# A cast of the last rows moved ahead of a slot's last exponentials, with other moves in the fill and the end, in a cross-attention kernel

## Chip, core and metric

The kernel runs on one core of one Trainium2 chip. The metric is the device time of one launch in microseconds (us). Engines are named as in the profile: PE (matmul) and PEld (its weight loads), DVE (vector), ACT (scalar), POOL (GpSimd) and SP, which here only issues DMAs.

## What is computed

For each of B = 32 pictures there are 512 query rows of 640 channels (x) and 77 context rows of 1024 channels. There are 20 heads of 32 channels, and the softmax runs over the 77 context rows (the reference has further branches for rows after the 77th; there are none here).

```python
q, k, v = heads(x @ wq), heads(ctx @ wk), heads(ctx @ wv)
p = softmax(q @ k.T / sqrt(32))
out = merge(p @ v) @ wo + bo + x
```

All is fp32. The kernel forms each product from pairs: a high part (a cast to the matmul's reduced fp32 type) and a low part (the value minus its high part), and adds three products, high x high, high x low and low x high.

## The kernel before

**Stages.** First all keys and values are computed from the context in five groups of columns (lines 294 to 383) and parked in DRAM (k_dram, v_dram). In the third of these groups the five blocks of the output weights wo are loaded, split into pairs and written to DRAM as pairs (split_wo, line 318); they are loaded again later (line 759). Then come N = 160 **slots** (slot, line 701): slot n = 5b + j treats four of picture b's heads (j = 0 to 4). Slots 1 to 7 are the **fill**, when no finished attention is there to be projected; from slot 8 on (has_out) every slot has the same load. Function end (line 845) drains the last pieces.

**One slot.** PE makes the scores of four row tiles (line 478; scores 0 to 3), the queries of the next slot (443), the attention product of slot n-4 (573: six passes, four ahead of scores 3 and two behind) and a piece of an earlier picture's output projection (622). DVE takes each score tile's negated maximum (486). ACT does 16 exponentials (496), four per score tile ("exps 0" to "exps 3"), each with its sum. Then:

- sums (506, DVE) takes the reciprocals; for j = 4, 0 and 1 it stands on DVE right behind exps 3, for j = 2 and 3 in the next slot. normalize (513, POOL) multiplies.
- transpose_p (520, DVE) transposes to z; four DMAs write z to pd in DRAM (527). load_p (536, 537) reads pd back, turned, as raw: one DMA of 512 KB for 256 of the 320 rows of probabilities, and one of 128 KB for the 64 **last rows**. load_p(n-3) is issued in slot n, and its raw is used in slot n+1.
- cast_p (544, 545, ACT) casts first the last rows, then the rest (128x1024; "the large cast") to the high parts pp; rest_p (551, DVE) and last_p (558, POOL) make the low parts. In the fill POOL does the large cast.
- copy_a (583, ACT) moves half of the attention product out of PSUM, add_a (588, DVE, two adds) sums it, high_a (599, ACT) and low_a (604, DVE) split the sum into the pair at, which the projection reads. copy_a and add_a of a product are in its own slot, around exps 3; high_a and low_a at the start of the next.
- split_q (454 ACT, 458 POOL, 460 DVE) splits the next slot's queries; split_x (263 ACT, 264 POOL) splits five blocks of the next picture's x in slots j = 2 and 3.
- finish (654, DVE) adds the projection to the residual xr, which frees one of two PSUM banks po, and sends full tiles to the output.

**What sets the order.** The order on each engine is the order of the calls in slot, written by hand (manual_schedule). Every engine, and SP's queue of DMA issues, works strictly in that order: an instruction that waits holds up all that stand behind it. Tiles with bufs=1 or 2 add waits for the last reader.

On ACT, a slot with j < 4 begins with last-rows cast, large cast, high_a, and ends with copy_a, exps 3. DVE ends it with sums, then add_a (where j = 4, 0 or 1). On SP, raw's two loads stand behind the four writes of pd and half of the loads of keys or values (refill).

Of the kernel before, what the change touches and what calls it, by code (L numbers as in the profile page):

```python
# [8 lines left out]
F32 = mybir.dt.float32  # L9
FPR = mybir.dt.float32r  # L10
# [41 lines left out]
def kernel(  # L52
# [46 lines left out]
    v_dram = dram.tile([NT + KPAD - NKEY, HPC, NC_, 3, HD], FPR, name="v_dram")  # L99
    wo_dram = dram.tile([P, NC_, 2, C], FPR, name="wo_dram")  # L100

# [3 lines left out]

    def load_weights(w, k0, kn, permuted=True, queues=(nc.sync,) * 4, tag="wraw"):


        raw = kvw.tile([P, 2, C], F32, tag=tag, name="wraw", bufs=3 if tag == "wraw" else 2)
        if permuted:  # L110
            rows = w.rearrange("(q c i) n -> q i c n", q=4, i=Q)
            for q, queue in enumerate(queues):
                queue.dma_start(raw[q * Q : (q + 1) * Q, :kn], rows[q, :, k0 : k0 + kn])
        else:
            rows = w.rearrange("(c p) n -> p c n", p=P)
            nc.sync.dma_start(raw[:, :kn], rows[:, k0 : k0 + kn])
        for k in range(kn):
            wraws[id(w), k0 + k] = raw[:, k]

    def split_weights(dst, w, k, scale=None):  # L120

        part = wraws.pop((id(w), k))
        if scale is not None:
            nc.scalar.mul(part, part, scale)
        split(dst[:, 0, :], dst[:, 1, :], part)
# [81 lines left out]
    def split_keys(g, j):  # L207
        g0, gn = GROUPS_KV[g]
        ks = kvt.tile([P, 2, G], FPR, tag="ks", name="ks")
        split(ks[:, 0, :gn], ks[:, 1, :gn], pks.pop(j)[:, :gn])  # L210
        engine = nc.gpsimd if g + 1 < len(GROUPS_KV) else nc.sync
        j0 = GROUPS[GROUP_OF[j]][0]
        engine.dma_start(
            k_dram[GROUP_OF[j]][:, :, j - j0, g0 : g0 + gn].bitcast(F32), ks[:, :, :gn].bitcast(F32)
        )
# [28 lines left out]

    def load_x(b, quarters=range(4), queue=nc.sync):

        if b not in xss:
            xss[b] = xpool[0].tile([P, S // Q, C // 4], F32, tag="xs", name="xs")
        xs = xss[b]
        src = x[b].rearrange("(a j) (q u) -> q j a u", j=Q, q=4)  # L250
        for q in quarters:
            queue.dma_start(xs[q * Q : (q + 1) * Q, :, :], src[q])

# [63 lines left out]

    def split_wo():
        k = len(split_ks) - NC_
        split_ks.append(k)  # L320
        ws = kvw.tile([P, 2, C], FPR, tag="ws", name="ws", bufs=2)
        split_weights(ws, wo, k)
        nc.sync.dma_start(wo_dram[:, k].bitcast(F32), ws.bitcast(F32))

    load_context(1, NK)
# [4 lines left out]
    for g in range(LAST):  # L330
        for j in range(NC_):
            if g or j > 2:
                values_of(g, j, psk)
            if not g and j < 3:
                split_keys(0, j)
            if not g and j == 2:
                continue
            if j == 1:
                context(g + 1, 0)
            if not g and j == 3:  # L340
                split_values(0, 2)
                split_keys(0, 3)
            if j == 3:
                continue
            if j == NC_ - 1:
                context(g + 1, 1, 2)
                if not g:
                    split_keys(0, 4)
                split_values(g, 3, (None, split_wq, split_wo, None)[g])
                context(g + 1, *range(3, NK))  # L350
                if g + 1 == LAST:
                    kvw.release()
                    kvc.release()
                    xpool.append(
                        ctx.enter_context(
                            tc.tile_pool(name="xpool", bufs=1, reuse_waits="tile")
                        )
                    )
                    load_x(0)
            split_values(g, j, (None, split_wq, split_wo, None)[g])  # L360
        if g + 1 < LAST:
            load_context(g + 2, NK)
            if g < 2:
                for k in range(0, NC_, 2):
                    load_weights((wq, wo)[g], k, min(2, NC_ - k), permuted=g == 0)
            for k in range(NK):
                for j in range(NC_):
                    keys(g + 1, j, k)
            for j in range(NC_):
                split_keys(g + 1, j)  # L370
# [3 lines left out]
    for c in range(NC_):  # L374
        split_x(0, c)
    load_x(1, queue=nc.gpsimd)

# [16 lines left out]

    bias = main.tile([P, C], F32, name="bias")
    kbs, vbs, pnb = [], [], []
# [8 lines left out]
    qts = [main.tile([P, 3, S], FPR, name=f"qt{n}") for n in range(2)]  # L405
    z = main.tile([P, NBLK, NQ, Q], F32, name="z")
    for g, (j0, nj) in enumerate(GROUPS):
        vb = main.tile([P, nj, 2, 2, P], FPR, name=f"vb{g}")
        vbs.append(vb)

# [10 lines left out]
    def copy_keys(g):  # L421
        kb = kbs[g]
        nc.gpsimd.tensor_copy(kb[:64, 0], kb[:64, 1].bitcast(F32))
        nc.gpsimd.tensor_copy(kb[64:, 3], kb[64:, 2].bitcast(F32))

    def load_values(b, g, segments=SEGMENTS):
# [90 lines left out]
    def transpose_p(n):  # L517

        pn = pnb[n % 2]
        nc.vector.transpose(  # L520
# [12 lines left out]
    def load_p(n):  # L533
# [4 lines left out]
        raws[n] = raw  # L538

    def cast_p(n, shared=False):  # L540

        raw = raws[n]
        pp = late[0].tile([P, 5, S], FPR, tag="pp", name="pp", bufs=1)
        nc.scalar.copy(pp[:64, 4, :], raw[:64, 2, :])  # L544
        (nc.gpsimd.tensor_copy if shared else nc.scalar.copy)(pp[:, 0:2, :], raw[:, 0:2, :])  # L545
        pps[n] = pp

# [66 lines left out]
    def add_bias(b, t):  # L614
        nc.gpsimd.tensor_tensor(xrs[b, t], xrs[b, t], bias, ALU.add)  # L615

# [59 lines left out]

    WO = {1: (0, 1, 2), 5: (3,), 6: (4,)}
    wos = []

    def take(m):  # L680
# [20 lines left out]
    def slot(n, beside=()):  # L701
# [9 lines left out]
        if not filling:  # L711
            refill(b, j, 0)
        copied = {1: 1, 4: 0 if more else None}.get(j)
        if copied == 0 and has_out:
            copy_keys(copied)
            copied = None
        if taken is not None and j != NC_ - 1:
            cast_p(taken, filling)
        if n - 1 in takes:
            high_a(takes[n - 1])  # L720
        if taken is not None and j == NC_ - 1:
            cast_p(taken, filling)
        bias_now = j in BIAS and b >= BIAS[j][0]
# [7 lines left out]
        if has_out and j in (1, 2):  # L731
            normalize(n - 1, rss.pop(n - 1))
        if taken is not None:
            last_p(taken)
        if copied is not None:
            copy_keys(copied)
# [11 lines left out]
        if j != NC_ - 1 and n - 1 in takes:  # L748
            low_a(takes[n - 1])
        if taken is not None:  # L750
            rest_p(taken)
        if n == LATE + 2:
            nc.sync.dma_start(bias, bo.unsqueeze(0).to_broadcast([P, C]))
        if n >= LATE:
            load_p(n - LAG + 1)
        if filling:
            refill(b, j, 0)
        for k in WO.get(n, ()):
            nc.sync.dma_start(wos[0][:, k].bitcast(F32), wo_dram[:, k].bitcast(F32))
        refill(b, j, 1)  # L760
# [3 lines left out]
        if j in RESIDUAL and b >= RESIDUAL[j][0]:  # L764
            load_residual(b - RESIDUAL[j][0], RESIDUAL[j][1])
        exps(n, 1, *s)
        for i in turns[0]:
            transpose_x(b + 1, i)
# [10 lines left out]
        if early:  # L779
            piece(bo_, first)  # L780
            if j == 4:
                values(taken, 0, 4)
                s3 = scores(n, 3)
                values(taken, 4, 6)
            finish()
        if not ahead:
            transpose_p(n - 1)
        if ahead:
            split_q(n + 1)
            if parted:  # L790
# [27 lines left out]
        else:  # L818
# [3 lines left out]
            if taken is not None:  # L822
                values(taken)
        if len(beside) > 0:
            context_values(LAST, beside[0], psv)
        finish()
        for i in turns[1]:
            transpose_x(b + 1, i)
        if taken is not None:
            copy_a(taken)  # L830
        for c in xsplits[1]:
            split_x(b + 1, c)
        exps(n, 3, *s)
        if has_out and j in (4, 0, 1):
            rss[n] = sums(n)
        if taken is not None:
            add_a(taken)
        if len(beside) > 1:
            context_values(LAST, beside[1], psv)
        if has_out:  # L840
# [4 lines left out]
    def end():  # L845
# [3 lines left out]
        load_p(N - 3)  # L849
        load_values(last, 1)  # L850
        load_residual(last - 1, 3)
        piece(last - 1, 4)
# [4 lines left out]
        last_p(N - 4)  # L857
        rest_p(N - 4)
        transpose_p(N - 1)
        add_bias(last - 1, 2)  # L860
        load_p(N - 2)
        piece(last - 1, 5)
# [73 lines left out]

    load_keys(0, 0)
    queries(0, 0, NC_)
    split_q(0)
    copy_keys(0)  # L940
    for vb in vbs:
        nc.gpsimd.memset(vb.bitcast(F32), 0.0)
    context_values(LAST, 0, psv)
# [56 lines left out]
```

## Time and profile before

| | us |
|---|---|
| median of 3 runs | 1950.41 |
| lowest, highest | 1945.75, 1954.95 |
| the profiled execution | 1956.04 |
| its span (first to last instruction) | 1954.3 |

The granted PE clock over the profiled span is 0.993 of full speed. In the profile's views a row of "waits" says which engine stood idle at which line, and what ended the idle time: total us, times, longest. A row of the timeline has start and length in us, engine, line and tiles; a bracket at its end is the idle time before it and what ended it. A row of the windows has the busy time of each engine, the granted PE clock and the share in which the DMA engines were busy.

### The profile page before, as it was taken

The page shows a single profiled execution, that of the slowest core. Times are in us where ns is not written, and L with a number is a line of the kernel's source. Part 1 is how long each engine was busy: PE and PEld are TensorE (multiplying, and loading weights), DVE is VectorE, ACT ScalarE, POOL GpSimd, SP SyncE. Part 2 cuts the span into 40 slices and gives each one's busy share as a digit, 9 for nine tenths or more (in the row PEclk, how much of TensorE's full clock was granted, in tenths as well). Part 3 has the DMA queues.
Part 4 walks back from the last instruction along what each step waited for, and adds up shares of the span by engine and source line. Part 5 has one row for each costly group of instructions (what it writes and reads, how often), then busy time and mean ns, then how long its engine had stood idle before and what let it go on. Part 6 is the DMA issues. An engine that isn't in the chain of part 4 may idle for free.

```text
span 1954.3 us, 37691 instructions
## 1 busy us (share of the span) xinstructions
PE 1902.4 (97%) x10332; PEld 1663.2 (85%) x10332; DVE 1638.7 (84%) x2494; ACT 1532.9 (78%) x6206; POOL 1376.5 (70%) x1264
## 2 busy tenths in 40 slices
PE   9999997999999999999999999999999999999998
PEld 7888886888888888888888888888888888888887
DVE  4444447899999989989999999999999999999995
ACT  3232247888899889888888888989988889889883
POOL 1000057888888888878888787888888888788874
PEclk9999998999999999999999999999999999999999
DMA  9878868898898988888888888988889898888875
GB/s 188 197 190 251 190 184 207 216 232 227 227 237 227 223 227 225 228 219 231 223 235 226 227 225 227 235 231 232 221 234 229 229 229 225 227 223 228 230 201 168
DMA packets 570657, 431.39 MB, mean 221 GB/s; under 512 B 199440, under 2 KB 479120, under 8 KB 570448
## 3 DMA queue, kind: packets, MB, share of 16 engines
q1 hardware_dynamic: 566832, 416.36, 84.6%
q0 software_dynamic: 3520, 12.45, 1.8%
q8 instruction: 86, 1.41, 0.3%
q14 instruction: 123, 1.01, 0.2%
q10 hardware_dynamic: 96, 0.16, 0.0%
HBM read 247.17 MB, written 181.64 MB: 219 GB/s over the span
## 4 chain that ended last, share of the span: by engine, by line
PE 43%; POOL 15%; DMA 13%; DVE 9%; ACT 7%; issue 7%; SPq 5%; POOLq 0%; DVEq 0%; ACTq 0%
PE po L622 11%; PE pq L443 11%; DMA raw<-pd 8%; PE pk L191 7%; PE pv L191 7%; POOL pn L513 5%; PE pa L573 4%; PE sc L478 4%; ACT pn L496 3%; POOL pp L558 3%; POOL qt L458 3%; POOL xt L264 2%; DMA xs<-in_x_dram 2%; DVE nm L486 2%; DVE pp L551 2%
## 5 line engine op out<-in xcount | busy, mean ns | idle before, releaser
L496 ACT ACTIVATE pn<-sc,nm 128x77 f32<-128x77 f32 x2560 | 794.3, 331 | 58.0 <-DVE nm L486 53.1
L622 PE MATMUL po<-wo_s,at 128*128 128x320 f32 x3840 | 629.1, 312 | 17.9 <-DVE xr L654 13.2
L443 PE MATMUL pq<-xt,wq_s 128*128 128x512 f32 x2400 | 631.5, 403 | 1.2
L622 PEld LDWEIGHTS po<-wo_s,at 128*128 128x128 f32 x3840 | 575.6, 188 | 47.8 <-DVE xr L654 26.5
L496 ACT ACTIVATION_READ_ACCUMULATOR pn<-sc,nm 128x1 f32 x2560 | 539.1, 211 | 0.0
L513 POOL TENSOR_TENSOR pn<-pn,rs 128x616 f32<-128x616 f32 x320 | 448.4, 1419 | 116.4 <-DVE rs L506 105.2
L443 PEld LDWEIGHTS pq<-xt,wq_s 128*128 128x128 f32 x2400 | 429.7, 191 | 85.8 <-POOL xt L264 10.8
L478 PEld LDWEIGHTS sc<-kb,qt 128*128 128x128 f32 x1920 | 327.2, 189 | 63.6 <-POOL qt L458 11.8
L478 PE MATMUL sc<-kb,qt 128*128 128x154 f32 (+1 forms) x1920 | 317.5, 273 | 16.4 <-POOL qt L458 7.7
L573 PE MATMUL pa<-pp,vb 128*128 128x512 f32 x960 | 295.7, 412 | 9.1 <-issue 5.1
L486 DVE TENSOR_REDUCE nm<-sc 128x4 f32<-128x308 f32 x640 | 285.6, 457 | 14.1 <-PE sc L478 9.3
L458 POOL CAST qt<-qt 64x512 fp32r<-64x512 f32 x320 | 194.9, 609 | 132.7 <-ACT qt L454 93.3
L551 DVE TENSOR_TENSOR pp<-raw,pp 128x1024 fp32r<-128x1024 f32 x160 | 272.3, 1702 | 14.2 <-ACT pp L545 11.9
L520 DVE STREAM_TRANSPOSE z<-pn 128x1280 f32<-128x1280 f32 x160 | 241.8, 1512 | 35.5 <-POOL pn L513 28.0
L558 POOL TENSOR_TENSOR pp<-raw,pp 64x512 fp32r<-64x512 f32 x160 | 207.0, 1294 | 56.8 <-ACT pp L544 44.6
L588 DVE TENSOR_TENSOR pa<-pa,aw 64x512 f32<-64x512 f32 x320 | 222.6, 696 | 14.6 <-ACT aw L583 4.1
L264 POOL TENSOR_TENSOR xt<-xs,xt 128x512 fp32r<-128x512 f32 x160 | 202.8, 1294 | 36.4 <-ACT xt L263 33.4
L460 DVE TENSOR_TENSOR qt<-pq,qt 64x512 fp32r<-64x512 f32 x320 | 218.6, 683 | 10.0 <-ACT qt L454 5.0
L615 POOL TENSOR_TENSOR xr<-xr,bias 128x640 f32<-128x640 f32 x128 | 203.2, 1588 | 12.4 <-PE sc L478 3.0
L573 PEld LDWEIGHTS pa<-pp,vb 128*128 128x128 f32 x960 | 160.3, 190 | 46.5 <-POOL pp L558 15.8
L544 ACT CAST pp<-raw 64x512 fp32r<-64x512 f32 x160 | 99.2, 620 | 101.2 <-DMA raw<-pd 97.4
L583 ACT COPY aw<-pa 64x1024 f32<-64x1024 f32 x160 | 162.0, 1013 | 19.2 <-PE pa L573 15.5
(47 smaller groups left out, 1656.5 us busy)
## 6 DMA issues: line engine op xcount, KB each, us to landing
pd<-z SPq DMA_DIRECT2D x640, 160.0 KB, 3.4
raw<-pd SPq DMA_DIRECT2D x160, 512.0 KB, 4.4
xr<-in_x_dram SPq DMA_DIRECT2D x128, 320.0 KB, 3.8
out_dram<-xr SPq DMA_DIRECT2D x127, 320.0 KB, 3.7
xs<-in_x_dram SPq DMA_DIRECT2D x124, 320.0 KB, 7.2
raw<-pd SPq DMA_DIRECT2D x160, 128.0 KB, 4.4
v_dram<-vs SPq DMA_DIRECT2D x80, 192.0 KB, 4.0
k_dram<-ks POOLq DMA_DIRECT2D x20, 512.0 KB, 4.7
```

What stands on the lines that cost most here:

```text
L191: nc.tensor.matmul(held[j][:, :gn], w[:, k, a, :], cts[g, k][:, c, :gn], start=(k == 0 and n == 0), stop=(k == NK - 1 and n == 2),)
L264: low.tensor_tensor(parts[1], src, parts[0].bitcast(F32), ALU.subtract)
L443: nc.tensor.matmul(pqs[n], wq_s[:, k, a, j * P : (j + 1) * P], xts[b, k][:, c, :], start=(k == 0 and m == 0), stop=(k == NC_ - 1 and m == 2),)
L458: nc.gpsimd.tensor_copy(qt[other, 1 + w, :], qt[r, 0, :].bitcast(F32))
L478: nc.tensor.matmul(sc[:, cols], qt[:, m, t * P : (t + 1) * P], keys_, start=(m == 0), stop=(m == 2),)
L486: nc.vector.tensor_reduce(nm, sc[:, :KCOLS].rearrange("p (h k) -> p h k", k=NKEY), AX.X, ALU.max, negate=True)
L496: nc.scalar.activation(pnb[n % 2][:, at, :NKEY], sc[:, i * NKEY : (i + 1) * NKEY], AF.Exp, bias=nm[:, i : i + 1], accum_out=sms[n][:, at : ...
L513: nc.gpsimd.tensor_tensor(pf, pf, rs[:, k : k + half].unsqueeze(2).to_broadcast([P, half, NKEY]), ALU.mult)
L551: nc.vector.tensor_tensor(pp[:, 2:4, :], raw[:, 0:2, :], pp[:, 0:2, :].bitcast(F32), ALU.subtract)
L558: nc.gpsimd.tensor_tensor(pp[64:, 4, :], raw[:64, 2, :], pp[:64, 4, :].bitcast(F32), ALU.subtract)
L573: nc.tensor.matmul(pas[n][:, p, :], vb[:, p, t, :], pp[:, c, :], start=(c == p), stop=(c == p + 2),)
L622: nc.tensor.matmul(pos[b, t, h][:, :HALF], ats[b * NC_ + j][:, a, t * P : (t + 1) * P], wos[0][:, j, c, h * HALF : (h + 1) * HALF], start= ...
```

## The change

**Slots.** The cast of the last rows becomes a function of its own, cast_rows. From slot 8 on it is called for the next slot, between copy_a and exps 3; the large cast stays in its slot, now behind high_a. For j = 4, high_a stood first already. In slots j = 4 the finish of the first projection piece moves ahead of scores 3.

**Fill.** wo is no longer split early: five raw blocks are loaded once (load_wo) into space of tiles that are allocated later (z, vb1, bias), and split in slots 1 (four) and 3 (one): high parts on ACT, low parts on POOL (two) and DVE (three). In slots 1 to 7 the casts and last_p move behind exps 1, rest_p behind exps 2, and load_p to the slot's start. The values of the last group are made in the slots as before, but their split stands behind exps 3. The last group's keys of heads j = 3 and 4 are written by ACT's queue instead of SP's; x of picture 1 is loaded by SP instead of POOL. vb1 is cleared in slot 2.

**End.** load_p(N-2) is issued ahead of the last value and residual loads and of the last transpose.

```diff
+    def cast_rows(n):
+        pps[n] = late[0].tile([P, 5, S], FPR, tag="pp", name="pp", bufs=1)
+        nc.scalar.copy(pps[n][:64, 4, :], raws[n][:64, 2, :])
     def cast_p(n, shared=False):
         raw = raws[n]
-        pp = late[0].tile([P, 5, S], FPR, tag="pp", name="pp", bufs=1)
-        nc.scalar.copy(pp[:64, 4, :], raw[:64, 2, :])
-        (nc.gpsimd.tensor_copy if shared else nc.scalar.copy)(pp[:, 0:2, :], raw[:, 0:2, :])
+        if n not in pps:
+            cast_rows(n)
+        (nc.gpsimd.tensor_copy if shared else nc.scalar.copy)(pps[n][:, 0:2, :], raw[:, 0:2, :])
...
-    WO = {1: (0, 1, 2), 5: (3,), 6: (4,)}
+    WO = {1: ((0, nc.gpsimd), (1, nc.vector), (2, nc.gpsimd), (3, nc.vector)), 3: ((4, nc.vector),)}
+    def split_wo(k, low):
+        hi, lo = wos[0][:, k, 0], wos[0][:, k, 1]
+        nc.scalar.copy(hi, wo_raw[k])
+        low.tensor_tensor(lo, wo_raw[k], hi.bitcast(F32), ALU.subtract)
...
         if not filling:
             refill(b, j, 0)
+        elif n >= LATE:
+            load_p(n - LAG + 1)
...
-        if taken is not None and j != NC_ - 1:
-            cast_p(taken, filling)
         if n - 1 in takes:
             high_a(takes[n - 1])
-        if taken is not None and j == NC_ - 1:
-            cast_p(taken, filling)
+        if taken is not None and not filling:
+            cast_p(taken)
...
-        if n >= LATE:
+        if n >= LATE and not filling:
             load_p(n - LAG + 1)
...
         exps(n, 1, *s)
+        if taken is not None and filling:
+            cast_p(taken, True)
+            last_p(taken)
+            if copied is not None:
+                copy_keys(copied)
+        for k in WO.get(n, ()):
+            split_wo(*k)
...
             if j == 4:
                 values(taken, 0, 4)
+                finish()
                 s3 = scores(n, 3)
                 values(taken, 4, 6)
             finish()
...
         if taken is not None:
             copy_a(taken)
-        for c in xsplits[1]:
-            split_x(b + 1, c)
+        if has_out:
+            for c in xsplits[1]:
+                split_x(b + 1, c)
+            if n + 1 in takes:
+                cast_rows(takes[n + 1])
         exps(n, 3, *s)
+        for c in beside:
+            split_values(LAST, c)
...
@@ end()
         load_p(N - 3)
-        load_values(last, 1)
-        load_residual(last - 1, 3)
         piece(last - 1, 4)
...
         rest_p(N - 4)
+        load_p(N - 2)
+        load_values(last, 1)
+        load_residual(last - 1, 3)
         transpose_p(N - 1)
         add_bias(last - 1, 2)
-        load_p(N - 2)
```

## Prediction

> **What bounds the kernel now.** I read the page's busy shares first, then the windows by stage.
>
> ```profile
> PE 1902.4 (97%) x10332; PEld 1663.2 (85%) x10332; DVE 1638.7 (84%) x2494; ACT 1532.9 (78%) x6206; POOL 1376.5 (70%) x1264
> ```
> ```profile
> 300.00:350.00 50.00, 36.54 (x145) 28.12 (x145) 38.38 (x57) 35.67 (x164) 38.10 (x37) 0.87 0.94 218
> 350.00:1850.00 1500.00, 1478.97 (x8331) 1301.82 (x8330) 1383.41 (x2102) 1335.02 (x5559) 1225.10 (x1112) 1.00 0.88 227
> ```
>
> From 350 to 1850 us PE idles 21 of 1500 us, so there is little to win; but DVE is busy 92% and ACT 89%, so there is little slack to lose. In the fill (300 to 350) PE idles 13.5 of 50.
>
> Next I measured slots on PE's timeline, from first score to first score. Over slots 10 to 154 the means for j = 0 to 4 are 9.83, 9.91, 9.95, 10.26 and 11.37: 51.3 us for five. The shortest are 9.81 to 9.85 for j < 4: there PE never waits. Then the waits:
>
> ```profile
> ACT pp L544 <- DMA raw<-pd: 97.4, 83, 4.1
> DVE at L604 <- ACT at L599: 55.4, 50, 4.8
> ACT at L599 <- DVE pa L588: 32.3, 34, 1.5
> PEld po L622 <- DVE xr L654: 26.5, 32, 0.9
> ```
>
> ACT's largest wait is for the raw rows, and it is met at the very cast that the change moves earlier. It matters what that cast is covered by now. ACT's timeline at the start of slot 61 (j = 1, begins 894.83), with the end of slot 60's exps 3 on top:
>
> ```profile
> 895.42 0.33 ACT L496 ACTIVATE pn<-sc,nm 128x77 f32<-128x77 f32 x1
> 895.62 0.21 ACT L496 ACTIVATION_READ_ACCUMULATOR pn<-sc,nm 128x1 f32 x1
> 897.08 0.62 ACT L544 CAST pp<-raw 64x512 fp32r<-64x512 f32 x1 [1.24 <-DMA raw<-pd]
> 897.61 1.05 ACT L545 CAST pp<-raw 128x1024 fp32r<-128x1024 f32 x1
> 898.56 0.58 ACT L599 CAST at<-pa 128x512 fp32r<-128x512 f32 x1
> 899.03 0.32 ACT L496 ACTIVATE pn<-sc,nm 128x77 f32<-128x77 f32 x1
> ```
> and DVE's:
> ```profile
> 895.87 0.25 DVE L506 RECIPROCAL rs<-sm 128x16 f32<-128x16 f32 x1
> 896.15 1.43 DVE L588 TENSOR_TENSOR pa<-pa,aw 64x512 f32<-64x512 f32 x2
> ```
>
> The exps end at 895.83; DVE takes 1.75 us from there to the end of the adds (897.58), which high_a needs. Now these 1.75 lie under the wait and the two casts; ACT loses nothing by them.
>
> **The steady slots.** No instruction is added or removed there; three are reordered. Slots 60 and 61, step by step:
>
> 1. The rows cast comes ahead of exps 3, at the time when raw lands: 897.08. Neither its load nor what stands before it on SP (writes of pd, half of refill) moves. It takes 0.53 (start to start), exps 3 take 1.33: they end at 898.94, 3.1 us later than before.
> 2. sums and add_a follow: 898.94 + 1.75 = 900.69. Only then can high_a run (0.47), then the large cast (0.95). The first exponential of slot 61 starts at 902.1, 7.3 us into the slot; before it was 4.2. Both covers are gone: one cast went ahead of the wait, one behind it.
> 3. What this costs PE is seen where raw once came late, in slot 56 (also j = 1):
>
> ```profile
> 845.32 0.62 ACT L544 CAST pp<-raw 64x512 fp32r<-64x512 f32 x1 [3.24 <-DMA raw<-pd]
> 847.27 0.32 ACT L496 ACTIVATE pn<-sc,nm 128x77 f32<-128x77 f32 x1
> ```
> ```profile
> 841.21 0.49 PE L478 MATMUL sc<-kb,qt 128*128 128x308 f32 x3
> ...
> 851.99 0.74 PE L478 MATMUL sc<-kb,qt 128*128 128x308 f32 x3
> ```
>
> The first exponential starts 6.06 into the slot, and the slot takes 10.78. In slot 11 it starts at 5.34 and the slot takes 10.05: past about 5.1, each us on ACT is a us on PE (the next queries' split comes too late). At 7.3 the slot takes 10.78 + 1.24 = 12.0, 2.1 over its mean.
>
> The other positions, by median landing after the slot's start (11.8, 12.2, 13.0, 11.4, 11.3 for j = 0 to 4) against the end of ACT's aw copy (9.5, 9.9, 10.8, 11.5, 10.5):
>
> - j = 2 follows a slot of 12.0, so its raw has landed; exps 3 of slot 61 end at 7.3 + 2.4 + 0.5 + 1.3 + 1.0 + 0.5 + 1.3 = 14.3, or 2.3 into slot 62; with 1.75 + 1.4 the first exponential starts at 5.5 and the slot takes about 10.0 (slot 92: 5.39, 9.91). Its mean is 9.95: +0.1.
> - j = 3: sums stands behind add_a, no 1.75; first exponential near 5.0, as now: 0.
> - j = 4: the same, less what finish brings. In slot 54 DVE ran two maxima (0.85) ahead of the adds that free po, and PE stood 0.44. One of the two is now behind: -0.4.
> - j = 0: the rows wait 0.9 in slot 4, exps 3 end 2.2 into slot 0, the first exponential starts at 5.4: +0.2.
>
> Sum: 2.1 + 0.1 + 0 - 0.4 + 0.2 = **+2.0 us for five slots, 30 times: +60**. Bounds: if half of step 1 is absorbed (SP has slack once slots are longer), slot 61's first exponential starts at 5.8 and the slot gains 0.6, with the other terms 0.5 in five slots: +15. If j = 2 and j = 0 lose as j = 1 does in its worst case, 4.0 x 30 = +120. I take +60, the step that slot 56 shows.
>
> The moved cast's wait depends on how long a small load takes. The page shows 4.4 us from issue to landing for the 128 KB load. The Trainium skill ("DMA: Bandwidth & Descriptors", Anatomy of one DMA) fits about 2 us plus the bytes over 436 GB/s, 2.3 us for this one; by that the rows would come 2.1 us sooner, hardly any wait would be left, and the steady sum would be an estimated +0 to +10. Here 88% of the DMA engines' time is taken, and the row decides.
>
> **Fill.** Removed: two passes of wo through DRAM, and ten split instructions from a stage where PE was busy 50.00 of 50 (150 to 200): no gain on PE. Added: four high casts in slot 1 at 0.73 (ws, line 103), 2.9 us on an ACT that worked 6 of 9.6 us there; POOL's lows at about 1.6 (nearest row: 128x640 at 1588 ns), DVE's at 0.78. PE did not idle in slots 1 to 3, so I price these at 0; if ACT's cover fails, at most +2.9. At 262.7 PE waited 2.33 for the first keys, queued on SP behind the last key store; that store moves to ACT: -2.3. In slots 4 to 7 PE idled 10.4, mainly for qt on POOL, which had waited 1.46, 1.49, 2.96 and 2.65 for raw at the large cast with normalize (2.4 to 3.5) still to do. Now normalize runs inside that wait: -5 (0 if raw is simply later, -8.6 if all of it goes). **Fill: -7, from -11 to +3.**
>
> **End.** The load of raw for N-2 stood behind eight value loads and four writes:
>
> ```profile
> 1921.38 0.56 SPq L536 DMA_DIRECT2D raw<-pd  x1
> ```
> ```profile
> 1930.08 2.52 PE L573 MATMUL pa<-pp,vb 128*128 128x512 f32 x6 [4.30 <-issue]
> ```
>
> It needs only its buffer, free at 1913.2 (rest_p); 8 us sooner it lands ahead of ACT. The pause of 4.30 goes; next late is DVE's rest_p, some 0.3. **-4, from 0 to -5.**
>
> **Sum.** Against the profile's own 1956.0: +60 - 7 - 4 = 2005. That execution lies 5.6 above the median of the runs, so the forecast is **1999 us**, 2.5% slower.
>
> **Rivals.**
>
> - *Faster.* If raw lands before ACT reaches the rows, nothing stalls. In slots j = 3 two thirds of the loads do (mean 0.2 ahead). Then the fill's -7, the end's -4, finish's -0.44 x 31 = -13.6 remain, and some of the 55.4 in which DVE waits for high_a: some 8. 1950 - 33 = **1917**. For: high_a sits behind both casts now. Against: the landing comes 0.8 to 2.4 us after the aw copy at four positions of five. It decides where that wait is shorter than about 0.5.
> - *No net change.* Slots of j = 1 lose under 1 us, since ACT idles 0.4 to 1 in most slots; the lower bound's +15 is eaten by fill, end and finish: **1945 to 1960**.
> - *Much slower.* A late z writes pd late, and this delays raw two slots on: a loop of rows, exps, adds, split, transpose, write, load. In slots 60 to 62 it runs 5.0 us from rows to split (897.08 to 902.05), 3.9 on to the end of z (905.96) and some 10.7 to the landing after next: 19.6 of the 19.7 us of two slots. 3.1 more on it, with only 1.2 taken back by a freer SP, would be +4 in five slots: **about 2060**.
>
> **How the numbers follow.** Forecast's mechanism, 1960 to 2050: 0.65. Much slower: 0.07. No net change (within 0.5%, 1940.7 to 1960.2, about what a measurement of this kernel can tell): 0.08. Faster: 0.20. The range runs from 1930, leaving out the larger part of the faster case, to 2055, near the upper bound.
>
> **What would show it.** ACT's wait for raw at the cast of the last rows stays or grows, now ahead of exps 3; a new wait of high_a for DVE's adds, near 1.7 us at j = 0, 1, 2; slots of j = 1 near 12 us; no PE pause near 1930; PE's wait for xr at j = 4 gone; POOL's waits for raw in slots 4 to 7 halved. I am wrong if slots j = 1 stay under 10.2, or if the rows hardly wait.

## The result, and the profile after

The changed kernel takes 2069.86 us (median of 4 runs, 2064.62 to 2079.16), the kernel before 1950.01 beside it: 1.062 times as long, 95% interval 1.057 to 1.067. The forecast was 1999, with 2055 as the upper end. Direction and place were right; the size was not.

Busy shares, then the two windows, in the order in which the kernel before was read:

```profile
PE 1945.1 (94%) x10332; PEld 1665.7 (81%) x10332; DVE 1616.8 (78%) x2492; ACT 1536.2 (74%) x6206; POOL 1376.1 (67%) x1262
```
```profile
300.00:350.00 50.00, 38.43 (x146) 29.39 (x145) 36.31 (x56) 35.77 (x171) 37.65 (x37) 0.82 0.88 204
350.00:1850.00 1500.00, 1418.17 (x7776) 1216.60 (x7775) 1271.75 (x1962) 1249.72 (x5183) 1143.09 (x1039) 1.00 0.84 212
```

From 350 to 1850 us PE idles 82 us instead of 21, and finishes 7776 matmuls instead of 8331; no other engine became the bound, all are less busy. The waits (total, times, longest):

```profile
ACT at L593 <- DVE pa L582: 168.1, 94, 3.1
...
ACT pp L533 <- DMA raw<-pd: 92.7, 83, 2.9
...
PEld po L616 <- DVE xr L648: 34.8, 85, 1.6
```

ACT's wait for raw is as long as before (97.4), but now it lies ahead of exps 3; high_a's wait for the adds is five times its 32.3. DVE's wait for high_a fell from 55.4 to 10.2. The end chain says it most plainly: shares by engine, first of the kernel before, then of the changed one.

```profile
PE 43%; POOL 15%; DMA 13%; DVE 9%; ACT 7%; issue 7%; SPq 5%; POOLq 0%; DVEq 0%; ACTq 0%
```
```profile
PE 22%; DMA 19%; ACT 19%; POOL 13%; DVE 12%; SPq 8%; issue 7%; POOLq 0%; ACTq 0%; DVEq 0%
DMA raw<-pd 12%; ACT pn L485 10%; PE pk L186 6%; PE pv L186 6%; POOL pn L502 4%; PE po L616 3%; PE pq L432 3%; DVE pa L582 2%; POOL xt L259 2%; ACT pp L533 2%; SPq L518 2%; PE pa L567 2%; DMA xs<-in_x_dram 2%; POOL qt L447 2%; SPq L404 2%
```

PE's share halves; raw's transfer (8% before) and the exponentials (3%) lead now. ACT's timeline in slot 61 (begins at 934.34), the slot that the forecast walked through:

```profile
937.57 0.62 ACT L533 CAST pp<-raw 64x512 fp32r<-64x512 f32 x1 [2.52 <-DMA raw<-pd]
938.20 0.33 ACT L485 ACTIVATE pn<-sc,nm 128x77 f32<-128x77 f32 x1
...
941.31 0.59 ACT L593 CAST at<-pa 128x512 fp32r<-128x512 f32 x1 [1.78 <-DVE pa L582]
941.80 1.05 ACT L540 CAST pp<-raw 128x1024 fp32r<-128x1024 f32 x1
942.74 0.33 ACT L485 ACTIVATE pn<-sc,nm 128x77 f32<-128x77 f32 x1
```

Steps 1 and 2 run as forecast: rows when raw lands, exps 3 behind it, 1.78 for reciprocals and adds, then high_a, the large cast, and the first exponential 8.4 us into the slot.

Where the 111.3 us went (span 1954.3 to 2065.6), from the starts of the slots in both traces:

| | forecast | measured |
|---|---|---|
| slots 10 to 154, 29 rounds of five: 51.32 to 54.94 | +2.0 each | +3.62 each, +105 |
| of it j = 0, 1, 2, 3, 4 | +0.2, +2.1, +0.1, 0, -0.4 | +0.32, +2.33, +1.44, -0.12, -0.36 |
| start of slot 0 | -2.3 | -3.0 |
| slots 0 to 9 (104.7 to 111.7) | -5 | +6.9 |
| slots 155 to 158 | with the steady | +3.1 |
| from slot 159 to the end | -4 | -0.4 |

Of what the forecast lacked, the steady slots are some 47 us, slots 0 to 9 some 12, and the last slots with the end some 5.

### The profile page after: what moved, and what is told of

The parts are those of the page before. It is cut to its first block, busy times and chain, and to the rows that moved or that the text cites. A ratio compares the mean times of both kernels' runs of the same rounds, so it can differ in the third digit from the quotient of the medians.

```text
span 2065.6 us, 37721 instructions
## 1 busy us (share of the span) xinstructions
PE 1945.1 (94%) x10332; PEld 1665.7 (81%) x10332; DVE 1616.8 (78%) x2492; ACT 1536.2 (74%) x6206; POOL 1376.1 (67%) x1262
## 4 chain that ended last, share of the span: by engine, by line
PE 22%; DMA 19%; ACT 19%; POOL 13%; DVE 12%; SPq 8%; issue 7%; POOLq 0%; ACTq 0%; DVEq 0%
DMA raw<-pd 12%; ACT pn L485 10%; PE pk L186 6%; PE pv L186 6%; POOL pn L502 4%; PE po L616 3%; PE pq L432 3%; DVE pa L582 2%; POOL xt L259 2%; ACT pp L533 2%; SPq L518 2%; PE pa L567 2%; DMA xs<-in_x_dram 2%; POOL qt L447 2%; SPq L404 2%
## 5 line engine op out<-in xcount | busy, mean ns | idle before, releaser
L485 ACT ACTIVATE pn<-sc,nm 128x77 f32<-128x77 f32 x2560 | 803.4, 350 | 27.8 <-DVE nm L475 24.2
L616 PE MATMUL po<-wo_s,at 128*128 128x320 f32 x3840 | 642.6, 314 | 14.8 <-DVE xr L648 9.0
L485 ACT ACTIVATION_READ_ACCUMULATOR pn<-sc,nm 128x1 f32 x2560 | 588.1, 230 | 0.0
L502 POOL TENSOR_TENSOR pn<-pn,rs 128x616 f32<-128x616 f32 x320 | 442.5, 1401 | 190.0 <-DVE rs L495 162.0
L467 PE MATMUL sc<-kb,qt 128*128 128x154 f32 (+1 forms) x1920 | 331.7, 277 | 28.8 <-ACT pn L485 17.0
L545 DVE TENSOR_TENSOR pp<-raw,pp 128x1024 fp32r<-128x1024 f32 x160 | 240.4, 1502 | 18.5 <-ACT pp L540 8.5
L593 ACT CAST at<-pa 128x512 fp32r<-128x512 f32 x160 | 94.3, 589 | 168.4 <-DVE pa L582 168.1
```

What stands on the lines that cost most here:

```text
L467: nc.tensor.matmul(sc[:, cols], qt[:, m, t * P : (t + 1) * P], keys_, start=(m == 0), stop=(m == 2),)
L485: nc.scalar.activation(pnb[n % 2][:, at, :NKEY], sc[:, i * NKEY : (i + 1) * NKEY], AF.Exp, bias=nm[:, i : i + 1], accum_out=sms[n][:, at : ...
L502: nc.gpsimd.tensor_tensor(pf, pf, rs[:, k : k + half].unsqueeze(2).to_broadcast([P, half, NKEY]), ALU.mult)
L545: nc.vector.tensor_tensor(pp[:, 2:4, :], raw[:, 0:2, :], pp[:, 0:2, :].bitcast(F32), ALU.subtract)
L616: nc.tensor.matmul(pos[b, t, h][:, :HALF], ats[b * NC_ + j][:, a, t * P : (t + 1) * P], wos[0][:, j, c, h * HALF : (h + 1) * HALF], start= ...
```

## The experiments

The theory at the start was the forecast's, called **lost cover**: the moved casts no longer lie over the reciprocals and adds that high_a needs. Its rival, **late raw**: holding exps 3 until raw lands is the cost, in whatever order the casts follow. The kernel before took medians of 1938 to 1954 us beside the five groups of runs, so runs are compared by their ratio to it on the same chip. "Five slots" is the mean length of five slots (j = 0 to 4) from 10 to 154; it moves with the chip too: 51.3 in the profile of the kernel before, 50.6 in that of e7, whose ratio is 1.001. Differences under about 0.7 between chips say nothing.

**The two steady moves, one by one** (e1, e2, e3; base: the changed kernel).

```diff
 e1, e3: rows in their own slot
-            if n + 1 in takes:
-                cast_rows(takes[n + 1])
 e1, e2: high_a behind the casts for j < 4
+        if taken is not None and j != NC_ - 1 and not filling:
+            cast_p(taken)
         if n - 1 in takes:
             high_a(takes[n - 1])
-        if taken is not None and not filling:
+        if taken is not None and j == NC_ - 1 and not filling:
             cast_p(taken)
```

> Base: the changed kernel. Both steady reorders undone: the last rows are cast in their own slot again, and high_a stands behind both casts for j < 4. Fill, end and the sooner finish stay as changed. Theory (the two reorders together took away the cover of DVE's reciprocals and adds, and this alone is the steady loss): five slots from 54.9 back to about 50.9 us, that is 51.3 of before less 0.4 of finish; slots 0 to 9 stay near 111 us; total about 1945. Rival 'elsewhere' (the loss comes from finish, the store that changed queue or the fill's late start, which run through the steady slots): five slots stay above 53 us, total over 2010.

> Base: the changed kernel; high_a stands behind the large cast again for j < 4, the rows are still cast a slot sooner. Theory (lost cover): the large cast (0.95) lies over the adds again, high_a's wait falls from 1.78 to about 0.8; first exponentials at 6.7 (j = 1), 4.9 (j = 2) and 4.9 (j = 0) into the slot; slots j = 0, 1, 2 of about 9.9, 11.3 and 10.0; five slots 52.4, total about 1995. Rival 'late rows' (the wait for raw ahead of exps 3 is the whole cost, the order behind it is nothing): as the changed kernel, 54 to 55 in five slots, about 2060. Rival 'order' (high_a first is the whole cost): 51, about 1945.

> Base: the changed kernel; the rows are cast in their own slot again, behind high_a and ahead of the large cast. Theory (lost cover needs both moves): exps 3 are not held up, the adds end about 2.75 us into slots j = 1 while raw lands at 2.4, so high_a first costs some 0.4 there and the first exponential starts at 4.7, under the 5.1 from which PE waits; five slots 50.9 to 51.3, total about 1947. Rival 'order': five slots near 54, total over 2030. Rival 'late rows': 51, as the theory; e2 tells these two apart.

| | ratio to before | five slots |
|---|---|---|
| e1, neither | 1.005 (1.003 to 1.007) | 51.21 |
| e2, rows sooner | 1.062 (1.059 to 1.065) | 54.55 |
| e3, high_a first | 1.029 (1.027 to 1.031) | 52.73 |
| the change, both | 1.062 (1.057 to 1.067) | 54.94 |

The steady loss is the two moves', not the fill's. But e2 goes against lost cover: with the large cast over the adds again the loss stays whole. ACT's timeline of e2 in slot 61 (begins at 934.16):

```profile
939.19 1.06 ACT L540 CAST pp<-raw 128x1024 fp32r<-128x1024 f32 x1
941.08 0.59 ACT L593 CAST at<-pa 128x512 fp32r<-128x512 f32 x1 [0.84 <-DVE pa L582]
942.18 0.33 ACT L485 ACTIVATE pn<-sc,nm 128x77 f32<-128x77 f32 x1 [0.51 <-DVE nm L475]
```

High_a's wait halves, as expected, but the first exponential is hardly sooner (8.0 us into the slot): now it waits for its maxima, which stand on DVE behind the same reciprocals and adds (and a transpose of x):

```profile
939.34 0.25 DVE L495 RECIPROCAL rs<-sm 128x16 f32<-128x16 f32 x1 [2.83 <-ACT pn L485]
939.63 1.42 DVE L582 TENSOR_TENSOR pa<-pa,aw 64x512 f32<-64x512 f32 x2
940.96 0.83 DVE L251 STREAM_TRANSPOSE xs<-xs 128x640 f32<-128x640 f32 x1
941.72 0.81 DVE L475 TENSOR_REDUCE nm<-sc 128x4 f32<-128x308 f32 x2
```

What follows from exps 3 is late whatever ACT does meanwhile. e3 missed too: I had it at no loss. There high_a waits 228 us in all ahead of the rows cast, so the low part of the last rows on POOL comes late, and PE stands 0.91 us for it in every slot j = 4 (12.52 us). This is a loss of its own: ACT never waits for raw at the rows in e3.

**The adds ahead of the reciprocals** (e4), on DVE.

```diff
-        if has_out and j in (4, 0, 1):
-            rss[n] = sums(n)
         if taken is not None:
             add_a(taken)
+        if has_out and j in (4, 0, 1):
+            rss[n] = sums(n)
```

> The changed kernel with one swap on DVE: add_a stands ahead of the reciprocals (sums) of the same slot, so that the adds need only ACT's copy and no longer exps 3. Theory (lost cover): high_a's wait of 1.78 for the adds goes at j = 4, 0, 1; first exponentials at about 5.9, 4.6 and 4.1 for j = 1, 2, 0; slots of about 10.6, 9.95 and 9.85; five slots 51.6, total about 1970. Rival 'late rows': the wait for raw ahead of exps 3 stays the cost, five slots stay above 53.5, total over 2030.

1.043 (1.039 to 1.046), five slots 53.64: nearer to late raw. High_a's wait falls from 168.1 to 37.3, but ACT's wait for raw grows from 92.7 to 133.9:

```profile
ACT pp L533 <- DMA raw<-pd: 133.9, 89, 3.8
...
ACT at L593 <- DVE pa L582: 37.3, 38, 3.8
```

A third of the 131 us that ACT gains behind raw it waits ahead of the next one.

**raw asked for sooner** (e5; e6 with e4's swap; e9 on e1, the old order).

```diff
+        if n >= LATE:
+            load_p(n - LAG + 1)
         if not filling:
             refill(b, j, 0)
```

> The changed kernel; on SP's queue load_p(n-3) stands at the start of slot n, ahead of the first half of refill (four key or value loads, some 3 us), instead of behind it. raw should land some 3 us sooner, about 9.5 us into the slot, where ACT reaches the rows at about 10.4. Theory 'late raw' (the wait for raw ahead of exps 3 delays all that follows from exps 3: reciprocals, adds, normalize, the low part of the last rows, the next maxima; the order of the casts is small): ACT's wait at the rows goes, five slots fall to 50 to 51, total about 1945. Rival 'lost cover': high_a still waits 1.78 at j = 0, 1, 2 with nothing over it, ACT then needs 10.7 us in these slots: five slots 52.5 to 53, total about 2000. Rival 'other' (neither): unchanged, 2060.

> The changed kernel with both: load_p at the slot's start on SP, and add_a ahead of the reciprocals on DVE. Both theories: neither the wait for raw nor that for the adds is left; the POOL chain behind exps 3 (normalize, low part of the last rows) is as early as before; five slots about 50, total 1915 to 1935. 'Late raw': within 10 us of the run with load_p alone; 'lost cover': over 40 us under it.

> The kernel of the first run (both steady reorders undone), with load_p at the slot's start on SP. raw lands 3 us sooner; before, ACT waits 97 us in all for it, mostly covered. Theory 'late raw': the first exponentials move up to 3.5 to 4.5 us, PE has no wait but in j = 3 and 4; five slots fall from 51.2 to 49.5 to 50.5, total 1910 to 1940. Rival: PE's own work (9.82 a slot, 10.3 and more with x's transposes) bounds, the wait was covered anyway: 51.2 stays, total 1955.

e5: 1.058 (1.056 to 1.060), e6: 1.046 (1.044 to 1.049), e9: 1.039 (1.036 to 1.041). As a tool this failed: counted from the slot's start, the last rows of raw landed 0.55 us sooner in e5 than in the changed kernel (mean 11.83 for 12.38), and 1.8 later in e9 than in e1 (14.1 for 12.3). The DMA issues of e9 (last column: median us from issue to landing; 4.6 for both in e1 and in the changed kernel):

```profile
raw<-pd SPq DMA_DIRECT2D x160, 512.0 KB, 6.2
...
raw<-pd SPq DMA_DIRECT2D x160, 128.0 KB, 5.8
```

Asked for right behind the writes of pd, the transfer took 1.2 to 1.6 us longer, in e5 as in e9. In e5 it was asked for 1.9 us sooner, in e9 not at all: there the whole refill, not half of it, stands between raw and the next writes of pd, and these began 2.4 us after z instead of 0.2. But e9 is worth keeping: the old order, with raw landing later, loses as well.

**The wait taken away by data** (e10; e11 with e4's swap): the sooner cast reads the raw of the product before.

```diff
-    def cast_rows(n):
+    def cast_rows(n, old=None):
         pps[n] = late[0].tile([P, 5, S], FPR, tag="pp", name="pp", bufs=1)
-        nc.scalar.copy(pps[n][:64, 4, :], raws[n][:64, 2, :])
+        nc.scalar.copy(pps[n][:64, 4, :], kept[n if old is None else old][:64, 2, :])
...
-                cast_rows(takes[n + 1])
+                cast_rows(takes[n + 1], taken)
```

> The changed kernel, but the sooner cast of the last rows reads the raw of the product before, which landed a slot earlier; same instruction, same place, no wait for the transfer just under way. What is left out: the high part of the last rows is that of another product. Moving the load on SP's queue did not bring raw sooner (it then took 5.9 to 6.3 us instead of 4.5 to 4.9), so this takes the wait away by data instead. Theory 'late raw' (the hold-up of exps 3 by raw, and with it of reciprocals, adds, normalize, low part and maxima, is the loss of the sooner cast): ACT's wait at the rows goes, and what stays is the price of high_a first, as in the run with that move alone: five slots 52 to 53, total about 1990. Rival 'order on ACT' (0.5 of cast ahead of exps 3 and the uncovered adds cost by themselves): five slots 54 to 55, total about 2055. Rival 'raw alone': 51.2, total about 1958.

> The run with the other raw, and add_a ahead of the reciprocals on DVE: neither the wait for raw nor high_a's wait for the adds is left in full. Both theories: five slots 50 to 51.3, total 1925 to 1960. If it stays over 53, the loss has a third cause that neither wait shows.

e10: 1.016 (1.015 to 1.018), five slots 51.61; e11: 1.001 (1.000 to 1.002), 50.67. ACT's longest wait in e10:

```profile
ACT at L595 <- DVE pa L584: 173.0, 97, 3.0
```

High_a waits as long as in the changed kernel, with the same order and the same casts; ACT has no wait for raw at the rows, and most of the loss is gone. By ratio, the two moves cost 5.7% (6.2 less the 0.5 of e1), and 1.1% stays (1.6 less 0.5); by five slots, 3.62 us, of which 1.0 stays over e7, which runs on the same chip as fast as the kernel before. That decides it for late raw. The rest is lost cover's: with the adds moved ahead (e11) it goes as well.

**Why a wait as long as before costs so much.** From the traces I took, for each product, the time from the end of z that precedes raw's issue to raw's landing, from there to the rows cast, and from the cast to the end of the next z but one, which precedes the raw of two slots on. The three close a loop of two slots (means over 140 products, us). They make up two slots by construction; what tells is which leg grows, and how much the middle one, the loop's slack, has left. Where ACT waits for raw it is 0.1.

```
                          z to landing   to rows cast   to z     two slots
before                        10.66          0.71        9.14      20.51
e1  neither                   10.70          0.65        9.14      20.49
e2  rows sooner               10.36          0.40       11.07      21.83
e3  high_a first              10.37          2.44        8.28      21.09
e4  adds first                10.55          0.38       10.54      21.46
the change                    10.40          0.37       11.22      21.98
e14 rows sooner but j = 1     10.54          0.78       10.44      21.76
e9  old order, later raw      12.26          0.25        9.08      21.59
e10 other raw                 10.44         -1.07       11.28      20.65
```

The loop had 0.71 us of slack. Rows and their wait ahead of exps 3 lengthen its last leg by 2.1; 0.34 of the slack takes some, 0.26 is a quicker landing, and the remaining 1.47 per two slots is 3.7 per five. e9 lengthens the first leg instead and loses too. In e3 the loop has 2.44 us to spare: its loss is none of the loop's. In e10 the cast no longer depends on this landing: the last leg is as long as ever, and costs almost nothing.

**One position spared** (e14): no sooner cast in slots j = 0.

```diff
-            if n + 1 in takes:
+            if n + 1 in takes and j != 0:
```

> The changed kernel, except that in slots j = 0 the rows of the next product are not cast sooner (they are cast in slot j = 1, behind high_a); j = 1 is where the stall of 3 us was forecast. 'Carry': j = 1 falls from 12.2 to about 10.2 and j = 2, which inherits no delay, to 10 to 10.4; five slots about 51.6, total about 1965. 'Each position by its own raw': j = 2's raw lands 13 us after slot j = 1 began, 2.8 us into slot j = 2 once j = 1 is 10.2 long; ACT now waits there, j = 2 takes about 12, j = 3 inherits; five slots 53 to 54, total 2010 to 2040.

1.051 (1.048 to 1.053), five slots 54.34. j = 1 falls from 12.24 to 10.46, and j = 2 rises from 11.39 to 13.15. The stall is not that of one position: spared at one, it appears at the next.

**Finish alone** (e7; base: the kernel before).

```diff
                 values(taken, 0, 4)
+                finish()
                 s3 = scores(n, 3)
```

> The kernel before with one change: in slots j = 4 the finish of the first projection piece stands ahead of scores 3. The forecast took 0.44 us a slot for it, 31 times. If PE's wait for xr is lost time: 1936, ratio 0.993. If the next slots give it back (in the first run j = 4 was 0.29 shorter, j = 1 to 3 together 0.2 longer): 1945 to 1950, ratio 0.998 to 1.

1.001 (1.000 to 1.002): nothing. Slots j = 4 take 11.08, and PE's matmuls do not wait for xr there, against 11.37 in the kernel before (profiled on another chip), yet the whole is not faster.

**Fill and end** (e8 on e1; e15 and e16 on the changed kernel).

```diff
 e8: blocks 2 and 3 of wo split behind split_q; the fill's casts, low parts and load_p back in their old places; in end:
         load_p(N - 2)
-        load_values(last, 1)
         load_residual(last - 1, 3)
+        load_values(last, 1)
 e15:
-        low.tensor_tensor(lo, wo_raw[k], hi.bitcast(F32), ALU.subtract)
+        nc.sync.dma_start(lo.bitcast(F32), hi.bitcast(F32))
 e16: load_wo("z", 0, 1), load_wo("vb1", 2) and load_wo("bias", 3) moved behind slot(0, (2,))
```

> The kernel of the first run (both steady reorders undone), with three things changed in the fill and the end. (a) wo: blocks 2 and 3 are split behind split_q of slot 1, both lows on POOL; blocks 0 and 1 where they were, lows on DVE. If the pause of 2.5 us at the second slot's scores is POOL's queue (two lows of 2.1 us each ahead of the query copies), slots 1 and 2 together fall from about 25.4 to about 23. (b) the casts of the fill back to the slot's start, as before: if moving them only shifted PE's pauses from the queries to the attention product, slots 4 to 8 stay within 57 to 59 us. (c) end: the load of the last residual but four ahead of the eight value loads instead of behind them: if the pause near 2040 us of the changed kernel (3.1 us) comes from that load, it goes and the stretch from the last slot to the end falls from 56 to 53. Total about 1950, 9 under the first run.

> The changed kernel, with the low parts of wo left out: a DMA copies the high part into the low part's place, so DVE and POOL have none of the five subtractions (1.1 us each on DVE, 2.1 on POOL); ACT's five high casts stay. 'The lows': slots 1 and 2 fall from 25.9 together to 20 to 21.5. 'Order of the values' split and the keys' copy in the fill': they stay above 24.

> The changed kernel, with the four first loads of wo issued behind slot 0 on SP (behind the eight stores of values and the key loads), not ahead of it. 'The stores' (DVE's first work of slot 1 waits 4.1 us for a store of values that comes late behind 1.3 MB of wo): that wait shrinks to under 2, the first exponential of slot 1 starts 2 us or more sooner, slots 1 and 2 together fall from 25.9 to 22 to 24 (wo then comes late itself). 'The splits' own work': 25 to 26 stays.

Totals 1.003 (1.001 to 1.005), 1.061 (1.059 to 1.064) and 1.056 (1.052 to 1.059). The casts: slots 4 to 8 take 53.7 in e8 and 59.2 in e1, so casting and loading later in the fill costs 5.5 us; 2.5 of it is idle time of PE, the rest goes with a lower granted clock (0.83 for 0.87). In the changed kernel these slots take 57.9, in the kernel before 56.8. There PE waited 7.7 us for POOL's qt; now it waits 7.7 for POOL's pp. Slots 1 and 2 took 19.3 before, and after:

```profile
271.48:282.99 11.51, 9.67 (x52) 8.85 (x52) 5.21 (x8) 6.08 (x22) 5.42 (x6) 1.00 0.68 142
282.99:297.43 14.44, 11.64 (x52) 10.08 (x52) 12.16 (x19) 9.30 (x51) 9.08 (x9) 0.88 0.50 110
```

Moving two splits (25.5) or leaving out all lows, with five DMAs on SP in their place (25.2), gave back almost nothing of the 6.7 lost. DVE's and SP's timelines in the changed kernel show what comes ahead of the splits:

```profile
273.59 0.62 DVE L223 STREAM_TRANSPOSE vs<-pv 128x416 f32<-128x416 f32 x1 [4.10 <-DMA v_dram<-vs]
```
```profile
258.67 2.28 SPq L679 DMA_DIRECT2D wo_raw<-in_L_xattn_to_out_w_dram  x4
261.00 2.12 SPq L247 DMA_DIRECT2D xs<-in_x_dram  x4
263.22 9.15 SPq L229 DMA_DIRECT2D v_dram<-vs  x8
```

The stores of the values, behind four blocks of wo and a picture's x, take 9.15 us to issue (5.3 before); DVE stands 4.1 for one of them, with slot 1's first maxima behind it. In e16, with wo behind the stores, that wait falls to 2.2 and the first exponential comes 1.9 us sooner, as early in the slot as in the kernel before; but wo now arrives late, ACT stands 4.1 for it at the high casts, and slots 1 and 2 take 28.9. Where wo's loads could lie at no cost I did not find, and how the 6.7 us divide among loads, stores and splits stays open.

The end: the changed kernel's pause on PE, its source on POOL, and the loads on SP.

```profile
2041.40 1.00 PE L567 MATMUL pa<-pp,vb 128*128 128x512 f32 x3 [3.11 <-issue]
```
```profile
2036.41 1.56 POOL L609 TENSOR_TENSOR xr<-xr,bias 128x640 f32<-128x640 f32 x1 [4.85 <-DMA xr<-in_x_dram]
```
```profile
2026.87 5.87 SPq L421 DMA_DIRECT2D vb<-v_dram  x8
2032.78 0.42 SPq L605 DMA_DIRECT2D xr<-in_x_dram  x1
```

raw(N-2) now comes in time (it lands at 2032.3, and ACT casts its rows at 2035.4 without a wait), but the residual stands behind the eight value loads in its place: POOL's bias waits for it, DVE's finish for the bias, the adds for finish. In e8 the residual goes first, and the next in line, the write of pd for raw(N-1), stands behind the eight. e8's pause, one attention product later:

```profile
1934.16 1.17 PE L567 MATMUL pa<-pp,vb 128*128 128x512 f32 x4 [3.56 <-DVE at L598]
```

4.30, 3.11, 3.56: one pause, handed on to whatever stands behind the eight loads. The changed kernel has another in slot 159 that belongs to the steady moves: exps 3, held up by raw, free the score bank late. It is 3.03 where the kernel before paused 0.88 and 1.09.

```profile
2013.21 0.60 PE L467 MATMUL sc<-kb,qt 128*128 128x308 f32 x3 [3.03 <-ACT pn L485]
```

**A version 0.3% faster** (e12; e13 is e12 without the swap). Base: the kernel before with e7's edit.

```diff
+        engine = nc.gpsimd if g + 1 < len(GROUPS_KV) else nc.sync if j < 3 else nc.scalar
...
         if n >= LATE:
             load_p(n - LAG + 1)
+        if not ahead:
+            load_values(b, 1)
...
-        load_values(last, 1)
         load_residual(last - 1, 3)
...
 e12 alone: add_a(taken) ahead of rss[n] = sums(n)
```

> The kernel before, with (a) the last keys of heads j = 3 and 4 stored by ACT's queue (about 3 us at the first scores), (b) the eight last value loads moved from the end into the last slot, where SP idles for some 10 us, so that none of raw, residual and pd stands behind them (the pause of 4.3 near 1930 us goes and does not move to the next transfer, as it did in two runs), (c) the sooner finish in j = 4, (d) add_a ahead of the reciprocals, which in the changed kernel took j = 4 from 11.0 to 10.2. Expected 1950 - 3 - 4 - 3 = 1940 if (d) gives nothing in the old order, 1920 if it gives 0.7 in five slots.

> The faster version without its fourth edit (add_a ahead of the reciprocals). In that version's profile j = 2 took 10.86, with PE waiting for the low part of the last rows on POOL, against 9.91 without the swap; j = 4 took 10.27 against 11.08. If the swap gives as much as it takes: ratio 0.996 to 0.997, as with it. If it costs 0.2 in five slots, as the two profiles have it: ratio 0.993.

e12: 0.997 (0.995 to 0.998), e13: 0.997 (0.995 to 0.998). Both beat the kernel before by 0.3%, little, but clear of the noise. In e12 slot 159 to the end takes 52.5 us instead of 56.7, with no pause over 1.5 left; PE idles 9.4 us there instead of 11.2, and the rest goes with the granted clock, 1.00 instead of 0.94. e13, with the same loads moved, has no pause over 1.7 either, but idles 11.1 in several short ones and takes 55.4: moving the eight loads broke up the pause, and only with the swap (one profile each) was there less idle time. In the slots the swap takes in j = 2 (10.86, 9.97 in e13) what it gives in j = 4 (10.27, 11.10).

## Why the prediction was right and wrong

- **Steps 1 and 2** (rows at the landing, high_a waiting 1.75 for the adds): right. The wait is 1.79 (168.1 over 94), slots j = 1 took 12.24 (forecast 12.0), their first exponential starts at 7.69 (7.3). But "both covers are gone" was not the cause: e2 gave one back and won nothing.
- **"j = 2: ... its raw has landed ... +0.1"** is the term that failed: +1.44 was measured. The first exponential starts at 6.51 there, not 5.5: slot j = 1 hands on 0.4 more and another 0.4 on its way to copy_a, ACT still waits 0.35 for raw, and the rest adds up from smaller pieces. The step from that to PE's loss, read from slot 56, held: it gives 11.2 for 6.51, and the slots took 11.39.
- **The step under it** priced raw's lateness position by position, each with a fresh landing. The runs showed a loop in its place: the landing hangs on the z of two slots before, that z on the exponentials, and these now on the landing. The rival "much slower" had this loop, with 19.6 of 19.7 us taken and +4 in five slots, 2060 in all; I gave it 0.07. It was the case: 3.62 in five slots; that the total agrees so well is in part luck, since that rival took the fill and the end as the forecast did, and they lost some 15 us against it. The profile had spoken for it: in 85 of 140 products the rows were cast within 0.2 us of raw's landing already, so the loop had next to no slack.
- **j = 0, 3 and 4** were right in size. But the -0.4 for finish is not shown to be earned time: alone it wins nothing (e7), and PE's matmuls now wait for xr in 11 slots j = 2, 0.77 us each.
- **Fill, -7**: wrong in sign. "Normalize runs inside that wait: -5" missed that PE then waits for the casts and low parts themselves, as long as it had for qt: +1.0 in slots 4 to 8, and +5.5 by e8. "PE did not idle in slots 1 to 3, so I price these at 0" counted the splits and left out wo's four loads ahead of the stores of values, though the DMAs of a moved step count too: +6.7, of which e16 shows the loads' part in the first exponential only. The key store on ACT's queue was right: -3.0 for 2.3 (e12 and e13 start as early).
- **End, -4**: the wait for raw(N-2) went, as forecast; what was late next was not rest_p (0.3) but the residual that the same edit put behind eight loads (a pause of 3.11 for 4.30). And the steady moves themselves cost slot 159 one more us of pause, which the sum did not hold.
- **The rule weighed**: the Trainium skill ("DMA: Bandwidth & Descriptors", Anatomy of one DMA) gives, for DMAs issued by GpSimd, an estimated 2.3 us for 128 KB. This load is issued by SP, and the profiles show 4.4 to 4.6 for it, and 5.8 in e9; the row was the better guide.

## What to carry to other kernels

Before a waiting instruction is moved ahead of other work, follow what that work feeds until it comes back to the awaited transfer, and add up the loop: with slack of 0.7 us in 20 every added us returns in every round, however short the wait looks. A wait total that stays the same says nothing of what stands behind it. On a queue that works in order, a pause cured by moving one transfer forward is handed to the one that takes its place; where possible move the long group (here eight value loads), and look whether idle time went or was only broken up (e12, e13).

## What the runs showed of the hardware

With its place on SP's queue moved forward, a transfer took longer: raw's 512 KB went from 4.6 us to 6.2 in e5 and e9, and the landing gained 0.55 us in e5 and lost 1.8 in e9. And a pause of PE can cost more than itself. In the kernel before, PE waits 2.33 us ahead of slot 0, and that slot runs at a granted clock of 0.85 and takes 11.03 us; with no wait, in the changed kernel, 1.00 and 9.47. Slot 2 of the changed kernel, with a pause of 2.47, has 0.88. The Trainium skill ("TensorE: Matmul & The Clock Gate", Part 1) has the clock fall to half after an idle window of about 3.4 us; here these shorter pauses of 2.33 and 2.47 were followed by a lower clock, while the pause of 1.52 in slot 61 left it at 1.00. Length alone does not decide it: in e4, of 23 pauses of 1.83 to 1.87 us, 11 were followed within 1.6 us by a stretch of 3.41 us at half clock and 12 were not, and in e8 a pause of 2.31 was not.
